# Pairing fewer edge chunks to a TensorE product in a graph layer, with two more spare products

## The chip, the cores and the metric

The kernel runs on one core of a Trainium2 chip. The metric is the device time of one execution in microseconds (us). Before the change, three runs took 308.38, 308.87 and 310.85 us; the median is 308.87. Engines are named as in the profile: PE is TensorE's matmul, PEld its weight load, DVE is VectorE, ACT is ScalarE, POOL is GpSimd, SP is SyncE.

## The reference

One layer of a graph network: 12,500 nodes of 128 numbers, 412,500 edges of 48 numbers, each edge added to its destination node, then a small MLP with a residual. The edges come sorted by destination.

```python
def reference(x, src, dst, edge_attr_48, graph_globals, W1, b1, W2, b2):
    h = jnp.maximum(_layernorm(x, axis=-1), 0.0)
    agg = jax.ops.segment_sum(edge_attr_48, dst, num_segments=12500)
    u = graph_globals[zeros(12500, int32)]
    z = jnp.concatenate([h, agg, u], axis=1)          # 128 + 48 + 64
    return x + jax.nn.relu(z @ W1 + b1) @ W2 + b2     # hidden 256
```

All is float32. Reading the edges' numbers takes most of the memory traffic: 412,500 x 48 x 4 bytes are 79 MB.

## The kernel before

**Steps.** The edges are cut into chunks of 896 (128 partitions x T = 7), and eight chunks make a step: two halves h of four chunks each. There are 58 steps, 0 to 57; the last has four chunks and a rest of 340 edges. Since the edges are sorted, the 896 destinations of a chunk lie within a window of 32 nodes. For each step VectorE builds a one-hot tile `oh` (`onehot`, line 290) that says for each edge which of the window's 32 nodes it belongs to, and `aggregate` (line 314) multiplies it with the edges on TensorE: for each of the seven t and each chunk one product of a 128x32 one-hot (the weights) with a 128x48 edge tile. The four chunks of a half write to four different groups of 32 of TensorE's columns. A step without pairs has 56 such products.

**Pairs, or levels.** `aggregate(s, h, twos)` can do the last `twos` of the seven t in another way: the one-hots of two neighbouring chunks, 64 columns, are the weights of one product, and both chunks' edges, 96 columns, stream through. Half of what comes out is of no use, the blocks off the diagonal. One such t is called a level here. A level takes two products in place of four, and each of them streams twice as many columns. Only the half h = 1 is ever paired. A step with at least one level needs two more copies in `keep_sums` (line 335), since the odd chunks' sums of that half then lie beside the even ones'; a step with no level needs one copy on ScalarE.

A product is recorded in the trace as two weight loads and two matmuls, as are the other float32 products.

**Loads.** Each step's edges come in four loads of two chunks, 336 KB, issued by SyncE (`load`, line 279), three steps ahead. `few` (line 272) lets at most FLIGHT = 5 loads (edges, node blocks and destinations) be under way, and also makes each load wait for the last TensorE product placed ahead of it in the program.

**The other work of a step.** `place` and `add` (lines 358 and 366) put a step's window sums, two steps later, at their nodes in the array `aggT`. The node blocks of 512 go through LayerNorm, a transposition (`turn`, `keep`), the two halves of the first product (`first_h`), its share from the aggregated edges (`first_a`), ReLU, the second product (`second`), the residual (`result`) and a store. These pieces are placed by hand in half steps k = 2s and 2s + 1 (`at`, `piece`), each with a reckoned TensorE time that `work[k]` adds up. The order on every engine is the order in which the program is written (`manual_schedule`).

**How many levels.** For each step, lines 770 to 777 reckon two times: `us`, the time that TensorE streams (1.75 plus the step's `work`, plus 0.08 for each level), and EACH_US for each product. `n` counts the products of the step, all kinds (57 to 70 before any pairing). Levels are added while the first time is the lower one, up to seven; the last four steps have none.

**Spare products.** `spare` (line 593) is a 128x128 by 128x512 product of constants whose result nobody reads. Two are issued before step 0, and one each in the half steps k = 1 and k = 3, that is, in steps 0 and 1.

**Order within a step** (lines 743 to 786): `place`, first load, pieces of 2s, second load, `add`, pieces of 2s + 1, third load, the aggregation of both halves, fourth load, `keep_sums`, and on VectorE the column positions of step s and the one-hots of step s + 2.

Of the kernel before, what the change touches and what calls it, by code (L numbers as in the profile page):

```python
# [22 lines left out]
def kernel(  # L23
# [117 lines left out]
    with fast:  # L141
# [34 lines left out]
        def product(*a, **k):  # L176
            count[0] += 1
            last[:] = [nc.tensor.matmul(*a, **k).ins.name]  # L178
# [100 lines left out]
        def load(s, i):  # L279
            if s >= NS or s == NSF and i > 1:  # L280
                if s == NSF and i == 2:
                    edges[s].append(etail)
                return
            for c in (2 * i,):
                e = ep.tile([P, 2, T * DE], F32, name="e")
                few(load_edges(e, s * CS + c, 2))
                edges.setdefault(s, []).extend([e[:, 0], e[:, 1]])
                both.setdefault(s, []).append(e)

        def onehot(s):  # L290
            oh = ohp.tile([P, CH, T, 2, W], F32, name="oh")

            def compare(to, n, r):
                nc.vector.tensor_tensor(  # L294
                    to, iota[:, None, :W].to_broadcast([P, n, W]), r[:, :, None].to_broadcast([P, n, W]), OP.is_equal)

            def chunks(a, b):
                compare(oh[:, a // 2:b // 2].rearrange("p c t u w -> p (c t u) w"), (b - a) * T,
                        rel[:, (s * CS + a) // 2:(s * CS + b) // 2].rearrange("p c t u -> p (c t u)"))

            if s == NSF:
                chunks(0, CH)
                compare(oh[:, CH // 2, :TT, 0], TT, relt[:, :TT])
            elif s < 2:
                chunks(0, CH)
                chunks(CH, CS)
            else:
                chunks(0, CS)
            onehots[s] = oh
# [4 lines left out]
        def aggregate(s, h, twos):  # L314
            left = s == NSF and h
            if h == 0:
                banks_s[s] = ps_agg.tile([P, 512], F32, name="ps")[:, :4 * DE].rearrange("p (h f) -> p h f", h=2)
            ps, es, oh = banks_s[s], edges[s], onehots[s]
            n = TT if left else T
            for t in range(n):  # L320
                first, end = t == 0 and h == 0, t == n - 1
                if t >= n - twos:
                    for q in range(0, CH, 2):
                        c = CH * h + q
                        product(ps[W * q:W * (q + 2), h], oh[:, c // 2, t], both[s][c // 2][:, :, t * DE:(t + 1) * DE],
                                start=first, stop=end, skip_group_check=True)
                    continue
                for q in range(1 if left else CH):
                    c = CH * h + q
                    o = DE * (q % 2) if twos else 0  # L330
                    product(
                        ps[W * q:W * (q + 1), h, o:o + DE], oh[:, c // 2, t, c % 2], es[c][:, t * DE:(t + 1) * DE],
                        start=first, stop=end, skip_group_check=True)

        def keep_sums(s, twos):
            ps = banks_s.pop(s)
            to = sums[s % NSB].rearrange("p h (u f) -> p h u f", u=2)[:, :, :, :DE]

            def keep_these(k, h, o):
                nc.scalar.copy(to[k, h], ps[k, h, None, o:o + DE].to_broadcast(  # L340
                    [k.stop - k.start, h.stop - h.start, 2, DE]))

            if s < NSF:
                keep_these(slice(0, P), slice(0, 2), 0)
            else:
                keep_these(slice(0, P), slice(0, 1), 0)
                keep_these(slice(0, W), slice(1, 2), 0)
            hs = [h for h in range(2) if twos[h]]
            for q in range(1, CH, 2) if hs else ():
                keep_these(slice(W * q, W * (q + 1)), slice(hs[0], hs[-1] + 1), DE)  # L350

        def place_columns(s):
            po = ohp.tile([P, 2, WP], F32, name="place")
            nc.vector.tensor_tensor(po, iota[:, None, :WP].to_broadcast([P, 2, WP]),  # L354
                                    pos[:, s, :, None].to_broadcast([P, 2, WP]), OP.is_equal)
            places[s] = po

        def place(s):
            banks_p[s] = pp = ps_p.tile([P, 512], F32, name="pp")
            po = places.pop(s)  # L360
            for h in range(2):
                k = W if s == NSF and h else P
                product(pp[:HI + DE, SECOND * h:SECOND * h + WP], sums[s % NSB][:k, h, :HI + DE], po[:k, h],
                                 start=(h == 0), stop=(h == 1), skip_group_check=True)

        def add(s):
            _, v = nc.values_load_multi_w_load_instructions(
                at_i[0:1, s:s + 1], engines=[DVE], min_val=low(s), max_val=high(s),
                skip_runtime_bounds_check_because="clamped to these on the chip")
            to = aggT[:, ds(v[0], WG)]  # L370
            nc.vector.tensor_tensor(to, to, banks_p.pop(s)[:HI + DE, :WG], OP.add)  # L371
# [186 lines left out]
        with tc.manual_schedule():  # L558
# [71 lines left out]
            def at(k, f, *a):  # L630
                todo.setdefault(max(0, k), []).append((f, a))


            def placed(s):
                return min(s + 2, max(LATE, s + 1))
# [48 lines left out]
            for j in range(NBL):  # L684
                k = where["turn", j]
# [13 lines left out]
            def apart(k, f, *a):  # L699
                while k - 1 in taken or k in taken or k + 1 in taken:  # L700
                    k -= 1
                taken.add(k)
                at(k, f, *a)
                return k
# [6 lines left out]
            at(6, middles, 1)  # L711
            at(10, check_dst, 0)
            at(12, check_dst, 1)
            for k in (1, 3):
                at(k, spare)
            for i in range(2, len(parts)):
                need = 2 * (parts[i][0] // CS - (4 if i == len(parts) - 1 else 0))
                k = apart(need - 4, middles, i)
                at(k + 2, check_dst, i)
                k = apart(k - 1, spread_dst, i, 1)  # L720
                k = apart(k - 1, spread_dst, i, 0)
# [5 lines left out]
            k = apart(2 * (NS - 6), verdict)  # L727
# [10 lines left out]
                at(where["turn", j], keep, j)  # L738
            assert placed(ready[x1]) < NS

            ALL, TURN, MORE, EACH_US = 1.75, 0.15, 0.08, 0.08
            counted = count[0]
            for s in range(NS):
                now = [p for p in range(NS) if placed(p) == s]
                paced[:] = [s] * (s > 0)

                def next_load(i):
                    if s > 0:
                        load(s + AHEAD - 1, i)

                if s < LATE:
                    for p in now:
                        place(p)
                next_load(0)
                for f, a in todo.pop(2 * s, []):
                    f(*a)
                next_load(1)
                if s < LATE:
                    for p in now:
                        add(p)  # L760
                for f, a in todo.pop(2 * s + 1, []):
                    f(*a)
                next_load(2)
                if s >= LATE:
                    for p in now:
                        place(p)
                        add(p)


                us = ALL + work.get(2 * s, 0.0) + work.get(2 * s + 1, 0.0)  # L770
                n, twos = count[0] - counted + CS * T, [0, 0]
                while us + TURN < EACH_US * n and twos[1] < T and s < NS - 4:
                    twos[1] += 1
                    us += MORE
                    n -= 2
                aggregate(s, 0, twos[0])
                aggregate(s, 1, twos[1])
                counted = count[0]
                next_load(3)
                keep_sums(s, twos)  # L780
                if s == 1:
                    place_columns(0)
                if s > 0:
                    place_columns(s)
                if s + EARLY < NS:
                    onehot(s + EARLY)
# [166 lines left out]
```

## Time and profile before

The profiled execution is one run under the hardware profiler.

| | |
|---|---|
| median of three runs | 308.87 us (308.38 to 310.85) |
| the profiled execution's own time | 310.81 us |
| its span in the trace | 309.1 us |
| mean granted TensorE clock | 0.994 of full speed |
| HBM read, written | 87.74 MB, 6.40 MB |
| packets of kind "instruction" on q8 | 51, 0.84 MB |
| edge loads | 230 |

Times in the trace count from the span's start. A row of the timeline merges neighbouring instructions of a kind: start, length, engine and line, names and shape of the first, and their number; in square brackets stands the engine's idle time ahead of it and what ended it. In the groups by line, the columns after the count are busy time, mean length of one in ns, and the idle time ahead with its releasers. "issue" is idle time for which the profile shows no wait. In windows, each engine has its busy time and number of instructions, and the last three columns are the granted clock, the share of time that the 16 DMA engines are busy, and GB/s. Nearly all products on the chip come through one helper, line 178, so groups are told apart by their tiles: `ps<-e,oh` is the aggregation, `pp<-place,sums` the placing, `ph` the first product, `po` the second, `pt` the transpositions.

Where the steps lie: step 24's aggregation starts at 129.30 us, step 51's at 264.31, step 53's at 273.75, step 57's at 293.24.

### The profile page before, as it was taken

How to read it: one execution, taken by the hardware profiler on the slowest of the kernel's cores; microseconds unless marked ns; L12 is line 12 of the kernel's file. 1: busy time of each engine (PE TensorE's matmuls, PEld its weight loads, DVE VectorE, ACT ScalarE, POOL GpSimd, SP SyncE). 2: the span in 40 equal slices, each digit the busy share in tenths (PEclk: the TensorE clock that was granted, in tenths of full speed). 3: DMA queues.
4: the chain of work that ended last, by engine and by line, in shares of the span. 5: the costliest groups of instructions: out<-in, count | busy, mean ns of one | idle time of the engine just before them, and what ended most of it. 6: DMA issues, size and time to landing. Idle time of an engine off the chain costs nothing. (4 is left out here: it accounts for less than half of the span.)

```text
span 309.1 us, 14799 instructions
## 1 busy us (share of the span) xinstructions
PE 291.4 (94%) x6397; PEld 227.5 (74%) x6398; DVE 231.8 (75%) x530; ACT 164.1 (53%) x426; POOL 78.5 (25%) x87
## 2 busy tenths in 40 slices
PE   7888999999999999989999999999999899999982
PEld 3577767767877877866877887876887777786772
DVE  6867958987695967759976598779984899797221
ACT  2223696465564764645454487655452884665320
POOL 8221041032120544222134204123303033223000
PEclk9997999999999999999999999999999999999999
DMA  7999999999999999999999999999999999998102
GB/s 231 313 322 316 338 338 336 343 361 296 336 344 333 365 349 331 312 333 287 319 354 326 363 335 333 346 348 322 315 367 312 289 354 321 375 357 279 39 0 75
DMA packets 69717, 95.15 MB, mean 308 GB/s; under 512 B 5018, under 2 KB 64611, under 8 KB 69647
## 3 DMA queue, kind: packets, MB, share of 16 engines
q1 hardware_dynamic: 67439, 87.53, 85.3%
q0 software_dynamic: 2208, 6.63, 5.6%
q8 instruction: 51, 0.84, 1.1%
q14 instruction: 19, 0.16, 0.1%
HBM read 87.74 MB, written 6.40 MB: 305 GB/s over the span
## 5 line engine op out<-in xcount | busy, mean ns | idle before, releaser
L178 PE MATMUL ps<-e,oh 128*32 128x48 f32 (+1 forms) x5288 | 117.6, 218 | 7.2 <-issue 4.6
L178 PEld LDWEIGHTS ps<-e,oh 128*32 128x32 f32 (+1 forms) x5288 | 100.7, 116 | 31.4 <-issue 10.2
L294 DVE TENSOR_TENSOR oh<-iota,rel 128x1792 f32<-128x1792 f32 (+1 forms) x60 | 116.0, 1936 | 0.0
L340 ACT COPY sums<-ps 128x192 f32<-128x192 f32 (+1 forms) x165 | 43.1, 262 | 97.5 <-PE ps L178 94.9
L497 POOL DMA_DIRECT2D out_dram<-ot x25 | 14.0, 560 | 207.9 <-DVE ot L489 156.1
L371 DVE TENSOR_TENSOR aggT<-aggT,pp 112x246 f32 x58 | 23.7, 409 | 39.6 <-PE pp L178 30.3
L411 POOL TENSOR_TENSOR xb<-xt,b_sb 128x512 f32<-128x512 f32 (+2 forms) x26 | 46.5, 1792 | 15.3 <-DMA xt<-in_x_dram 9.8
L178 PE MATMUL po<-w,hid 128*128 128x128 f32 (+1 forms) x384 | 47.7, 276 | 1.3 <-ACTq L815 1.3
L178 PE MATMUL ph<-hT,w1h 128*128 128x512 f32 (+2 forms) x100 | 47.5, 578 | 0.6 <-ACT hT L432 0.6
L178 PEld LDWEIGHTS po<-w,hid 128*128 128x128 f32 (+1 forms) x384 | 44.9, 191 | 2.2 <-ACTq L815 1.4
L475 ACT ACTIVATE hid<-ph,bias 128x512 f32<-128x512 f32 (+2 forms) x49 | 30.4, 670 | 24.5 <-PE ph L178 23.3
L418 ACT ACTIVATE xn<-xt,sh,sc 128x128 f32<-128x128 f32 (+1 forms) x98 | 40.5, 483 | 0.5
L178 PE MATMUL pp<-place,sums 128*112 128x128 f32 x232 | 39.7, 295 | 0.0
L178 PEld LDWEIGHTS pp<-place,sums 128*112 128x112 f32 x232 | 29.2, 178 | 7.6 <-issue 1.5
L354 DVE TENSOR_TENSOR place<-iota,pos 128x256 f32<-128x256 f32 x58 | 34.3, 593 | 0.0
L178 PE MATMUL ph<-aggT,w1a 48*128 48x256 f32 (+1 forms) x192 | 28.3, 400 | 0.0
L432 ACT COPY hT<-pt 128x512 f32<-128x512 f32 (+2 forms) x26 | 26.7, 1026 | 3.1 <-PE pt L182 3.1
L489 DVE TENSOR_TENSOR ot<-po,xb 128x512 f32<-128x512 f32 (+2 forms) x25 | 16.6, 665 | 13.5 <-PE po L178 12.2
L178 PEld LDWEIGHTS ph<-aggT,w1a 48*128 48x128 f32 x192 | 17.3, 186 | 10.9 <-issue 7.8
L388 DVE BATCH_NORM_STATS2 st<-xt 128x6 f32<-128x128 f32 (+1 forms) x98 | 21.3, 279 | 1.8 <-DMA xt<-in_x_dram 1.8
L178 PEld LDWEIGHTS ph<-hT,w1h 128*128 128x128 f32 x100 | 16.2, 191 | 6.4 <-issue 3.3
L182 PE MATMUL pt<-ident,xn 128*128 128x128 f32 (+1 forms) x98 | 15.9, 282 | 0.0
(120 smaller groups left out, 139.7 us busy)
## 6 DMA issues: line engine op xcount, KB each, us to landing
e<-in_edge_attr_dram SPq DMA_DIRECT2D x230, 336.0 KB, 5.1
xt<-in_x_dram SPq DMA_DIRECT2D x23, 256.0 KB, 4.8
out_dram<-ot POOLq DMA_DIRECT2D x23, 256.0 KB, 5.5
di<-in_dst_dram SPq DMA_DIRECT2D x3, 448.0 KB, 6.9
xt<-in_x_dram SPq DMA_DIRECT2D x2, 128.0 KB, 4.2
out_dram<-ot SPq DMA_DIRECT2D x2, 128.0 KB, 2.6
di<-in_dst_dram SPq DMA_DIRECT2D x1, 154.0 KB
w1h<-in_L_gnn_W_dram POOLq DMA_DIRECT2D x1, 128.0 KB, 5.6
```

What stands on the lines that cost most here:

```text
L178: last[:] = [nc.tensor.matmul(*a, **k).ins.name]
L182: last[:] = [nc.tensor.transpose(*a, **k).ins.name]
L294: nc.vector.tensor_tensor(to, iota[:, None, :W].to_broadcast([P, n, W]), r[:, :, None].to_broadcast([P, n, W]), OP.is_equal)
L340: nc.scalar.copy(to[k, h], ps[k, h, None, o:o + DE].to_broadcast([k.stop - k.start, h.stop - h.start, 2, DE]))
L354: nc.vector.tensor_tensor(po, iota[:, None, :WP].to_broadcast([P, 2, WP]), pos[:, s, :, None].to_broadcast([P, 2, WP]), OP.is_equal)
L371: nc.vector.tensor_tensor(to, to, banks_p.pop(s)[:HI + DE, :WG], OP.add)
L388: nc.vector.bn_stats(st[:m, q, :], xs[j][:m, q, :])
L411: nc.gpsimd.tensor_tensor(xb[:m, :r], xs[j][:m, :r], b2_sb[:m, None, :].to_broadcast([m, r, D]), OP.add)
L418: nc.scalar.activation(xn[:m, q], xs[j][:m, q], AF.Relu, bias=shift[j][:m, q:q + 1], scale=scale[j][:m, q:q + 1])
L432: nc.scalar.copy(hT[:, :m * r].rearrange("d (p r) -> d r p", r=r), ht[j][:, :m * r].rearrange("d (r p) -> d r p", r=r))
L475: nc.scalar.activation(to, ph, AF.Relu, bias=bias[:, h:h + 1])
L489: nc.vector.tensor_tensor(ot[:m, :r], pos_o[j][:m, :r], xbs[j][:m, :r], OP.add)
```

## The change

```diff
@@ the spare products
-            for k in (1, 3):
+            for k in range(1, 8, 2):
                 at(k, spare)
@@ the plan of levels
-            ALL, TURN, MORE, EACH_US = 1.75, 0.15, 0.08, 0.08
+            ALL, TURN, MORE, EACH_US, FEW = 1.75, 0.15, 0.08, 0.073, 3
...
                 us = ALL + work.get(2 * s, 0.0) + work.get(2 * s + 1, 0.0)
                 n, twos = count[0] - counted + CS * T, [0, 0]
                 while us + TURN < EACH_US * n and twos[1] < T and s < NS - 4:
                     twos[1] += 1
                     us += MORE
                     n -= 2
+                if twos[1] < FEW:
+                    twos[1] = 0
                 aggregate(s, 0, twos[0])
                 aggregate(s, 1, twos[1])
```

The reckoned time of a product falls from 0.080 to 0.073 us, so that a step asks for fewer levels. A step that asks for one or two gets none. Spare products also go into the half steps 5 and 7, that is, steps 2 and 3. What is loaded, computed and stored stays the same, and so does every other piece's place.

## The prediction

> **What bounds the kernel now.** I read the page first: busy shares, slices, queues.
>
> ```profile
> span 309.1 us, 14799 instructions
> PE 291.4 (94%) x6397; PEld 227.5 (74%) x6398; DVE 231.8 (75%) x530; ACT 164.1 (53%) x426; POOL 78.5 (25%) x87
> PEclk9997999999999999999999999999999999999999
> DMA  7999999999999999999999999999999999998102
> q8 instruction: 51, 0.84, 1.1%
> e<-in_edge_attr_dram SPq DMA_DIRECT2D x230, 336.0 KB, 5.1
> ```
>
> TensorE is busy for 94% of the span, and the DMA engines are full in nearly every slice up to the 37th of 40, which ends at 286 us. Two resources are full at once, so the question is which one waits for the other. The groups by line, the windows, SyncE's own waits and the general waits answer that.
>
> ```profile
> L178 PE MATMUL ps<-e,oh 128*32 128x48 f32 (+1 forms) x5288 | 117.6, 218 | 7.2 <-issue 4.6 <-DMA e<-in_edge_attr_dram 2.5
> L340 ACT COPY sums<-ps 128x192 f32<-128x192 f32 (+1 forms) x165 | 43.1, 262 | 97.5 <-PE ps L178 94.9
> 180.00:220.00 40.00, 39.45 (x884) 31.19 (x880) 33.51 (x72) 24.37 (x62) 9.06 (x8) 1.00 1.01 338
> SPq L127 <- DMA e<-in_edge_attr_dram: 116.4, 179, 3.0
> SPq L127 <- PE pp L178: 5.7, 20, 0.4
> ```
>
> The loads run on their own clock. At most five are in flight (FLIGHT, line 556); five of 336 KB (344,064 bytes), landing in 5.1 us, make 337 GB/s, and the window from 180 to 220 us shows 338 with a DMA share of 1.01. SyncE waits for an earlier load 179 times, 116.4 us in all; its most frequent wait for TensorE is 20 times, never over 0.4 us. So a quicker TensorE does not make the edges arrive sooner. TensorE's aggregation in turn stood only 2.5 us on a missing load. Both streams move at nearly the same pace.
>
> At the end they part. The timeline of SyncE and TensorE there:
>
> ```profile
> 256.42 24.50 SPq L127 DMA_DIRECT2D e<-in_edge_attr_dram  x24
> ...
> 264.31 1.95 PE L178 MATMUL ps<-e,oh 128*32 128x48 f32 x92
> ...
> 273.75 2.11 PE L178 MATMUL ps<-e,oh 128*32 128x48 f32 x84
> 275.79 2.05 PE L178 MATMUL po<-w,hid 128*128 128x128 f32 x16
> ...
> 279.06 1.40 PE L178 MATMUL ps<-e,oh 128*32 128x48 f32 x112
> 280.39 1.13 PE L178 MATMUL ph<-hT,w1h 128*128 128x512 f32 x2
> ...
> 283.54 0.54 PE L178 MATMUL ps<-e,oh 128*32 128x48 f32 x30
> ...
> 284.64 1.12 PE L178 MATMUL ps<-e,oh 128*32 128x48 f32 x82 [0.56 <-issue]
> ...
> 293.24 0.80 PE L178 MATMUL ps<-e,oh 128*32 128x48 f32 x56
> ```
>
> The first row holds the last 24 of the 230 loads, one each 1.02 us. Four belong to a step and two to the last step, so number 207, issued at 256.42, is the third of step 51, and the fourth goes about 1.0 us later. With 5.1 us to landing the two are there at 261.5 and 262.5. TensorE begins step 51's products at 264.31. It needs the third and fourth load only for the half h=1, about 0.7 us into the block, so it could have begun at 261.8. It is 2.5 us behind the loads. The last load goes at about 256.4 + 24.5 = 280.9 and lands near 286, but step 57's products start at 293.24: after step 51 TensorE alone sets the end.
>
> **What the change does to TensorE's stream.** The plan (lines 741 to 785) can be worked out by hand. A common step has pieces of 2.68 us and 67 products. Its reckoned time is 1.75 + 2.68 = 4.43. Before, a level is added while the time + 0.15 is under 0.08 x products: 4.58 < 5.36, 4.66 < 5.20, 4.74 < 5.04, 4.82 < 4.88, then no more, so four levels. After, the bound is 0.073 x products: 4.58 < 4.89, 4.66 < 4.75, then no more. Two are under three, so none. Over the 58 steps this gives 288 levels in 53 steps before and 180 in 36 after. Of the 108 levels lost, 62 go from 17 steps that fall to none, and 46 from other steps, one to two levels each. Two of my counts have a check in rows above: 57 x 56 + 28 + 4 = 3224 products unpaired less 2 x 288 are 2648, four of them on the tail's own tile, and 2644 x 2 records are the 5288 shown; ACT's copies are 58 + 1 + 2 x 53 = 165.
>
> A level's price comes from three blocks with 84, 96 and 112 records, that is seven, four and no levels (56 products less two a level, two records each). The first and the last stand above. The four-level one, step 24, and the block after it:
>
> ```profile
> 129.30 1.87 PE L178 MATMUL ps<-e,oh 128*32 128x48 f32 x96
> 131.10 0.69 PE L178 MATMUL pp<-place,sums 128*112 128x128 f32 x4
> 131.63 1.02 PE L178 MATMUL ph<-hT,w1h 128*128 128x512 f32 x2
> 132.58 1.14 PE L178 MATMUL ph<-aggT,w1a 48*128 48x256 f32 x8
> 133.65 0.66 PE L182 MATMUL pt<-ident,xn 128*128 128x128 f32 x4
> 134.24 0.79 PE L178 MATMUL ps<-e,oh 128*32 128x48 f32 x53
> 135.94 1.34 PE L178 MATMUL ps<-e,oh 128*32 128x48 f32 x43 [0.92 <-issue]
> ```
>
> From a block's start to the next operation are 275.79 - 273.75 = 2.04 us with seven levels, 131.10 - 129.30 = 1.80 with four, and 280.39 - 279.06 = 1.33 with none. So a level costs TensorE 0.08 us (0.24 over three), and a block without any saves 0.15 more (0.47 over four levels). The stream gets shorter by 108 x 0.08 + 17 x 0.15 = 8.6 + 2.6 = 11.2 us.
>
> **What it adds: instructions.** Each lost level is two products more, 216 in all, and a product is two weight loads and two matmuls: 864 instructions, and 8 for the two spare products. The page has 6397 + 6398 such records against 51 packets of the kind "instruction" on q8, about 251 records and 16 KB to a packet; 872 more need about 3.5 packets more. That these packets can hold TensorE up is seen in the last fence: step 25's block stops for 0.92 us on "issue", that is, on nothing that the profile shows. The answer for 133.5 to 136.0 us, around that stop, counts one such packet, and the one for 131.0 to 133.5 none:
>
> ```profile
> q8 instruction: 1, 0.02, 2.3%
> ```
>
> ```profile
> 240.72 1.67 PE L178 MATMUL ps<-e,oh 128*32 128x48 f32 x51 [0.96 <-issue]
> PE ps L178 <- issue: 4.6, 9, 1.0
> ```
>
> In all the aggregation loses 4.6 us in nine stops. Without pairs a step of 67 products holds 268 instructions, more than one packet, 224 of them in 1.33 us, so every one of the 17 steps meets the end of a packet, many inside the dense block. What a step loses to this lies between nothing and the longest stop, 0.96 us (more instructions give no gain). Steps 52 and 54 to 57 already run without pairs and had one stop, 0.56 us (284.64): 0.11 a step. But their last ones run as the loads thin out, so I take 0.3, nearer to the tail's value than to the 0.96: 17 x 0.3 = 5.1 us. TensorE then gains 11.2 - 5.1 = 6.1 us gross (range: 11.2 down to 11.2 - 16.3 = -5.1).
>
> The Trainium skill, page "Runtime: NRT & Kernel Launch", section "Instruction fetch mechanics", says that instructions come in 16 KiB blocks of 256, that the next is fetched while the current one executes, and that crossing a boundary is mostly hidden. The packet size agrees; the stops of 0.92 and 0.96 us do not. By that rule alone the new instructions would be free, which is the first rival below.
>
> **How much of it reaches the end.** Not 6.1 us: up to step 51 TensorE can only close up on loads that do not come sooner. The most that can count is the 2.5 us by which it trails them there, and 0.08 from step 53 (seven levels to six): 2.6 us. Of that something is lost to stops too late to be made up. The surplus on the loads is small (6.1 us over some 46 steps, 0.13 a step), so a stop like that of 0.96 at 240.72, five steps ahead of step 51, is still mostly there, and steps 45 and 50, both newly without pairs, bring 0.3 each: 0.96 + 0.6 = 1.6 us. Left: 1.0 us.
>
> **What costs nothing.** ACT makes two copies fewer in 17 steps, 34 x about 0.26 = 8.9 us; its copies wait 94.9 us for TensorE, so nobody waits for them. The two spare products go into steps 2 and 3, late in each, ahead of its block and of its third load's place in the order:
>
> ```profile
> 13.92 1.13 PE L178 MATMUL ph<-iota,ones 128*128 128x512 f32 x2
> 14.97 1.49 PE L178 MATMUL ps<-e,oh 128*32 128x48 f32 x58
> ...
> 20.61 1.37 PE L178 MATMUL ps<-e,oh 128*64 128x96 f32 x26 [0.51 <-DMA e<-in_edge_attr_dram]
> ...
> 24.76 0.38 PE L178 MATMUL ps<-e,oh 128*64 128x96 f32 x2 [0.33 <-DMA e<-in_edge_attr_dram]
> 25.72 2.50 PE L178 MATMUL ps<-e,oh 128*64 128x96 f32 x26 [0.58 <-DMA e<-in_edge_attr_dram]
> ...
> 31.61 1.37 PE L178 MATMUL ps<-e,oh 128*64 128x96 f32 x26 [0.54 <-DMA e<-in_edge_attr_dram]
> ```
>
> One takes 14.97 - 13.92 = 1.05 us, two 2.1. TensorE waits for loads there 0.51 + 0.33 + 0.58 + 0.54 = 1.96 us, and the block at 25.72 takes 1.13 us longer than its like at 20.61, in the fourth slice, whose granted clock is 0.7 on the page; more work may hold it up: 3.1 us of cover. If the cover were gone, 2.1 us would push the steps behind, and the wait at 31.61 shows the loads still last there, so step 4 takes that up. The two loads of a step that are paced by the spare product (line 277) wait longer for an earlier load anyway.
>
> **The rivals.**
> *The instructions come free.* For it: the blocks at 279.06 and 293.24 ran without pairs and without a stop. Against it: nine stops before, with thinner blocks. Then the whole 2.6 us count: 308.87 - 2.6 = 306.3.
> *The supply of instructions becomes the bound: slower.* Place: the 17 steps without pairs. A four-level step with 67 products takes 134.24 - 129.30 = 4.94 us, and 4.47 without pairs if nothing stops it. If TensorE gets a packet's 64 products only every 5.1 us (0.08 us a product, the value the plan had), the step takes 67 x 0.08 = 5.36, 0.42 worse, and 17 x 0.42 = 7.1 us less the 46 x 0.08 = 3.7 of the other steps is 3.4 us slower: 312.3. It decides from 4.94 x 64 / 67 = 4.7 us a packet. For it: the stops near 1 us. Against it: step 54 went from 279.06 to 283.54, 4.48 us for 67 products, with loads still running.
> *Nothing moves.* The loads or stops take all back: 308.9.
> That the plan does something else is excluded by the changed program's list of products, where steps stand with 56 unpaired.
>
> **How the numbers follow.** The profiled execution took 310.81 us, 1.7 beyond its span, at the upper edge of the runs (308.38 to 310.85, median 308.87). The sum, made on it, is 310.81 - 1.0 = 309.8; its difference applied to the median gives 307.9, the forecast, with 0.5. Its own range is 306.6 to 309.2. Free instructions 0.17, supply-bound 0.2 (taking in milder forms from 309.5 on), nothing moves 0.13. The range, with two in ten outside, is 306.0 to 311.2. A measurement can tell about 1% from no change: faster means below 305.8, past the 2.6 us that the loads allow, so only a quicker load stream gives it: 0.08. Slower means above 312.0: 0.14, most of the supply rival. The same: 0.78.
>
> **What would show it.** Groups: 5288 + 432 = 5720 records of ps, 12 of the spares, 131 copies; q8 at 54 or 55. "PE ps <- issue" should grow from 4.6 us to 8 to 11, and TensorE's waits for e with it, as it closes up. Step 51's block should begin 0.5 to 2 us earlier against its loads, and the loads' last issue stay at 281. Wrong would be: a last load clearly earlier or later (the loads are not independent), issue stops unchanged (free instructions), or blocks without pairs that stop in nearly every step (supply-bound).

## The result: 2.7% slower

The changed kernel takes 319.03 us (median of six runs, 316.99 to 322.02) against 311.05 us (six runs, 308.38 to 312.48) for the kernel before. The ratio is 1.027, with a 95% interval of 1.020 to 1.033; it is that of the mean times, with one slow run of the changed kernel, 322.02, left out. The forecast was 307.9 and its range ended at 311.2. The rival in which the supply of instructions becomes the bound had the right sign, at 312.3, less than half the loss.

The page of the profile after, with the lines that answer to those shown of before:

```profile
span 317.1 us, 15643 instructions
PE 287.0 (91%) x6833; PEld 222.2 (70%) x6834; DVE 233.6 (74%) x530; ACT 155.0 (49%) x392; POOL 76.1 (24%) x87
PEclk9999999999999999999999999959999999999998
q8 instruction: 55, 0.90, 1.2%
L178 PE MATMUL ps<-e,oh 128*32 128x48 f32 (+1 forms) x5720 | 108.6, 215 | 14.6 <-issue 12.0
```

TensorE has 436 matmul records more and is busy 4.4 us less (291.4 before), in a span that is 8.0 us longer: it stands still more. The aggregation's idle time on "issue" went from 4.6 to 12.0 us. The waits for TensorE as a whole and SyncE's own:

```profile
PE ps L178 <- issue: 12.0, 12, 1.7
PE ph L178 <- issue: 2.3, 2, 1.3
PE pp L178 <- issue: 2.0, 1, 2.0
PE po L178 <- issue: 1.1, 1, 1.1
```

```profile
SPq L127 <- DMA e<-in_edge_attr_dram: 104.3, 157, 2.6
SPq L127 <- PE ps L178: 12.8, 14, 3.8
```

Matmuls that stand on "issue" come to 17.4 us in 16 stops; before there were nine, all in the aggregation. And the loads now wait for TensorE's aggregation 12.8 us, up to 3.8 us at a time. The same row of before, and the last 24 loads of after:

```profile
SPq L127 <- PE ps L178: 1.8, 8, 0.3
```

```profile
255.96 30.11 SPq L127 DMA_DIRECT2D e<-in_edge_attr_dram  x24
```

The 24 loads begin where they began before, at 256 us, and take 30.11 us in place of 24.50, so the last one goes at about 286 us in place of 281. TensorE fell behind the loads. Its own waits for edges did not grow (2.4 us, 2.5 before).

One stretch of the timeline, steps 38 and 39, shows the worst stop:

```profile
201.08 1.40 PE L178 MATMUL ps<-e,oh 128*32 128x48 f32 x112
202.41 0.36 PE L178 MATMUL pp<-place,sums 128*112 128x128 f32 x1
204.76 0.49 PE L178 MATMUL pp<-place,sums 128*112 128x128 f32 x3 [1.99 <-issue]
205.09 1.33 PE L178 MATMUL ph<-hT,w1h 128*128 128x512 f32 x2
206.35 2.08 PE L178 MATMUL ph<-aggT,w1a 48*128 48x256 f32 x8
208.36 1.11 PE L182 MATMUL pt<-ident,xn 128*128 128x128 f32 x4
209.40 2.47 PE L178 MATMUL ps<-e,oh 128*32 128x48 f32 x112
```

A block without pairs runs at full speed, 1.33 us from its start to the next operation, and one record after it TensorE stands for 1.99 us. What follows is slow: the same block at 209.40 takes 2.47 us for 1.40, the eight records of `ph` 2.08 us for 1.14. The windows give the granted clock, the third number from the right:

```profile
196.00:204.00 8.00, 6.77 (x223) 5.67 (x218) 6.44 (x15) 4.39 (x11) 2.66 (x2) 1.00 0.99 332
204.00:212.00 8.00, 7.24 (x130) 4.89 (x130) 4.17 (x8) 2.50 (x5) 0.41 (x1) 0.60 0.92 308
```

The clock falls to half after the stop and stays there for 6.8 us by the trace's clock records.

### The profile page after: what moved, and what is told of

It reads as the page before. It is cut to its first block, busy times and chain, and to the rows that moved or that the text cites. A ratio compares the mean times of both kernels' runs of the same rounds, so it can differ in the third digit from the quotient of the medians.

```text
span 317.1 us, 15643 instructions
## 1 busy us (share of the span) xinstructions
PE 287.0 (91%) x6833; PEld 222.2 (70%) x6834; DVE 233.6 (74%) x530; ACT 155.0 (49%) x392; POOL 76.1 (24%) x87
## 5 line engine op out<-in xcount | busy, mean ns | idle before, releaser
L178 PE MATMUL ps<-e,oh 128*32 128x48 f32 (+1 forms) x5720 | 108.6, 215 | 14.6 <-issue 12.0
L178 PEld LDWEIGHTS ps<-e,oh 128*32 128x32 f32 (+1 forms) x5720 | 93.4, 115 | 39.5 <-issue 19.8
L340 ACT COPY sums<-ps 128x192 f32<-128x192 f32 (+2 forms) x131 | 35.3, 270 | 104.2 <-PE ps L178 102.3
L411 POOL TENSOR_TENSOR xb<-xt,b_sb 128x512 f32<-128x512 f32 (+2 forms) x26 | 44.2, 1704 | 14.8 <-DMA xt<-in_x_dram 8.9
L354 DVE TENSOR_TENSOR place<-iota,pos 128x256 f32<-128x256 f32 x58 | 35.7, 616 | 0.0
L178 PE MATMUL ph<-aggT,w1a 48*128 48x256 f32 (+1 forms) x192 | 29.8, 412 | 2.3 <-issue 2.3
L178 PEld LDWEIGHTS ph<-aggT,w1a 48*128 48x128 f32 x192 | 18.3, 192 | 13.8 <-issue 10.6
```

The source lines that it names most:

```text
L411: nc.gpsimd.tensor_tensor(xb[:m, :r], xs[j][:m, :r], b2_sb[:m, None, :].to_broadcast([m, r, D]), OP.add)
```

## Where the time went, by a sum over the steps

Undisturbed pieces take the same time to about 0.01 us in all the kernels of the table: a block without levels 1.33 us, with two 1.64, four 1.80, seven 2.04, and the other work of a kind of step likewise. So the time from the start of step 5's aggregation to that of step 57's can be split in two: the stream (the undisturbed lengths added up) and what lies above it. One profile each, in us, worked out from the traces; "instructions" is the difference to the kernel before on TensorE, four a product, and "issue" the waits of all matmuls on issue over the whole span.

```
kernel            instructions  levels   stream  above it   issue (stops)   ratio to before (95%)
before                     0      288    250.5      7.0       4.6 (9)
changed                 +872      180    239.3     26.9      17.4 (16)     1.027 (1.020 to 1.033)
changed, again          +872      180    239.3     24.6      14.3 (18)     1.025 (1.015 to 1.036)
dense_only              +496      226    243.0     19.4      11.9 (16)     1.012 (1.004 to 1.020)
each_only               +640      208    243.8     18.9      14.6 (15)     1.008 (0.999 to 1.016)
even182                 +856      182    241.7     21.8      13.7 (21)     1.013 (1.008 to 1.019)
even182, again          +856      182    241.7     13.9       9.9 (11)     1.013 (1.005 to 1.020)
more_pairs              -512      352    255.7      2.6       1.5 (3)      1.010 (1.005 to 1.014)
merge_a                 -184      288    250.5      8.1       6.7 (8)      1.003 (0.999 to 1.007)
```

The change saved the 11.2 us of stream that were forecast and paid 19.9 us (17.6 in the second profile) above it. Within that part of the span the waits on issue grew from 4.3 to 17.4 us, by 13.1; the half clock of 6.8 us can add some 3.4 us (an estimate: half of that time). The rest is not accounted for one by one.

The stops have a signature. Number all of TensorE's instructions in the trace from 0: weight loads, matmuls and the rest, mostly waits on semaphores. Then the first instruction behind each of the changed kernel's 16 stops, a matmul or its weight load, has a number that leaves 193 when divided by 256. The same holds for all stops in the table's other profiles, though their products lie at other places. Each of the 16 ends 2.2 to 2.6 us after a 16 KB packet of kind "instruction" begins to move. So a stop is TensorE at the end of one packet's 256 instructions, waiting for the next. In the changed kernel the next packet begins to move 2.5 us (median) after TensorE has entered the one before, in the kernel before 2.2 us; with the some 2.4 us to its first use that makes 4.5 to 5 us to get 256 instructions. This time varies: at the 16 stops it was 4.5 to 7.0 us, with a median of 5.7.

Where the stops stand is not where the pairs went. Only 5 of the 16, 6.1 us, lie in the 17 steps that fell to none, and all of these come at the end of the dense block or behind it. From one aggregation's start to the next, those 17 steps together take 0.8 us more than before (0.8 less in the second profile), and the 35 other steps between 5 and 57 take 8.0 us more (7.3). Five of the stops in other steps stand in the step right behind one of the 17, so a step may use up a packet and leave the wait for the next one to the step behind it.

## Experiments

Theory S: the change makes TensorE use its instructions faster than packets of them come. Rival F: instructions come free, and the loss is in something else (spare products, clock, thinner pairs). Later S was split: S1, their number counts; S2, it counts how fast a single packet is used up.

**One part at a time.** dense_only:

```diff
+                if s in (6, 8, 9, 11, 13, 18, 20, 24, 25, 26, 32, 33, 38, 39, 40, 45, 50):
+                    twos[1] = 0
                 aggregate(s, 0, twos[0])
```

> The kernel before with one part of the change alone: the 17 steps that the change leaves without pairs have none, all other steps keep their levels (288 to 226 levels), no new spare products. Theory S (supply of instructions): 124 products more are 496 more TensorE instructions, all in dense blocks; the stops on issue in the aggregation grow from 4.6 us to 9 us or more, the stream saves only 17 x 0.31 to 0.47 = 7.5 us, and the time is 1 to 2% above the kernel before. Rival F (instructions come free, the slowdown is from something else, the spare products or the lower clock): 0.5 to 0.8% faster than before, stops unchanged.

315.16 us, ratio 1.012 (1.004 to 1.020): slower, as S has it, and the stops grew as forecast. The stream is 7.5 us shorter, the time above it 12.4 us longer.

```profile
PE ps L178 <- issue: 10.3, 14, 1.5
```

each_only:

```diff
-            ALL, TURN, MORE, EACH_US = 1.75, 0.15, 0.08, 0.08
+            ALL, TURN, MORE, EACH_US = 1.75, 0.15, 0.08, 0.073
```

> The kernel before with 0.073 in place of 0.080 us a product alone: 208 levels in 51 steps, no step set to none, no new spare products. It has 160 products more than before, 56 fewer than after, and the 17 steps keep one or two levels each. Theory S: still short of instructions, stops of 7 to 10 us, 0.5 to 1.5% slower than before. If setting the 17 steps to none is what hurts, apart from the number of instructions: equal to before within 0.3%. Rival F: 0.5 to 0.8% faster.

314.88 us, ratio 1.008 (0.999 to 1.016). The stops are above the forecast 7 to 10 us; the time is where S put it, its interval just reaching no change.

```profile
PE ps L178 <- issue: 12.9, 14, 2.2
```

spares_only:

```diff
-            for k in (1, 3):
+            for k in range(1, 8, 2):
```

> The kernel before with the two new spare products in steps 2 and 3 alone. Theory S and the prediction: within 0.4% of before, since the loads are last there; the granted clock stays full around 26 us where the kernel before shows a stretch at half. Rival (the spares push the early steps and this is never made up): 2 us or 0.7% slower.

311.74 us, ratio 1.001 (0.993 to 1.009): the spare products cost nothing that shows, and F loses that place. Around 26 us the clock is full, as expected, but not all along: the trace has half clock from about 15 to 18 us and from 32 to 35 us, the fifth slice of the page here (31 to 39 us) reading 0.7.

```profile
PEclk9989799999999999999999999999999999999999
```

**Do packets wait behind the loads?** after_flight3, the changed kernel:

```diff
-        FLIGHT = 5
+        FLIGHT = 3
```

> The changed kernel with at most 3 loads under way in place of 5. Theory S with the fetch waiting behind loads in the DMA engines: packets of instructions start sooner, stops fall from 12 us to 7 or less and TensorE closes up on the loads; if 3 loads still fill the DMA engines (load stream as long as before, last issue near 285 us), the time falls by 1.5 to 3% against the changed kernel, to 309 to 314 us. If the time to get a packet doesn't depend on the loads: stops stay at 12 us and the time is that of the changed kernel. If 3 loads are too few: TensorE waits for e over 10 us and the time is above 320.

389.31 us, ratio 1.25 (1.241 to 1.259): three loads are too few. The loads, in the page's part on DMA issues:

```profile
e<-in_edge_attr_dram SPq DMA_DIRECT2D x230, 336.0 KB, 4.2
```

and TensorE's waits:

```profile
PEld ps L178 <- DMA e<-in_edge_attr_dram: 67.8, 71, 2.5
```

A load lands in 4.2 us, less by 1.1 than the 5.3 with five in flight, so three bring 3 x 0.344 MB / 4.2 us = 246 GB/s. TensorE then waits for edges and has no stop on issue, so the time says nothing on packets. The trace says a little: the next packet begins to move 1.3 us (median) after TensorE enters one, against 2.5 in the changed kernel with five loads. That speaks for packets that wait behind loads, but TensorE's waits for edges shift the moment from which this is counted, so it is not shown. flight7, the kernel before with FLIGHT = 7, asks from the other side:

> The kernel before with 7 loads under way in place of 5. If a packet of instructions waits its turn behind the loads in the DMA engines, more loads in flight make every packet later: stops on issue grow from 4.6 to over 9 us and the time by 1 to 3%, while the loads come no faster, the engines being full already. If packets don't wait behind loads: stops and time as before, within 0.3%.

310.47 us, ratio 0.998 (0.994 to 1.002), 6.7 us of stops. SyncE's waits:

```profile
SPq L127 <- PE pp L178: 69.2, 76, 3.5
SPq L127 <- DMA e<-in_edge_attr_dram: 23.9, 45, 1.2
```

With seven allowed, the loads run up to where they must wait for TensorE, and the time does not move. The stops, 6.7 us, lie between the two forecasts, and the next packet begins to move 1.7 us (median) after TensorE enters one, not later than the 2.2 of before. So more loads in flight do not make the packets later by an amount that shows, and in the kernel before, too, it is TensorE, not the loads, that sets the time.

**The number of instructions with the stream held.** merge_a (the kernel before, levels written out as they were):

```diff
-            for q in range(0, n, 256):
-                w = min(256, n - q)
+            for q in range(0, n, 512):
+                w = min(512, n - q)
```

> The kernel before, with its levels held fixed, and each block's product with the aggregated edges done over 512 columns at once in place of twice 256: 46 products or 184 TensorE instructions fewer, the streamed columns the same. Theory S (time per instruction where the supply is short): from the first call the cost is about 11 to 23 ns an instruction (dense_only: 3.9 us slower with 7.5 us less stream for 496 instructions), so 2 to 4 us, of which the loads let about 2.5 us through: 0.5 to 0.8% faster than before, the stops fall below 4 us. Rival F (the number of instructions is not what counts, the thinner pairs are): equal within 0.2%.

312.72 us, ratio 1.003 (0.999 to 1.007): no gain. S as it stood, a price per instruction, missed.

split_h, its counterpart:

```diff
-            product(ph, w1h[:, h * P:(h + 1) * P], ht[j][:, :n], start=(h == 0 or not small),
-                             stop=False, skip_group_check=True)
+            for q in range(0, n, 256):
+                product(ph[:, q:min(q + 256, n)], w1h[:, h * P:(h + 1) * P], ht[j][:, q:min(q + 256, n)],
+                        start=(h == 0 or not small), stop=False, skip_group_check=True)
```

> The counterpart: the kernel before, its levels held fixed, and each block's first product over 256 columns twice in place of 512 once: 46 products or 184 TensorE instructions more, the streamed columns the same, and the weights of those products loaded twice. Nothing in the aggregation changes. Theory S: 2 to 4 us or 0.6 to 1.3% slower, and the stops on issue in the aggregation grow though the aggregation is untouched. Rival F: equal within 0.3%, stops as before.

313.81 us, ratio 1.010 (1.003 to 1.017). In this run part of the first product's sum is lost in the hidden layer; instructions and stream are as said. Slower as forecast, but not by the cause: the stops did not grow.

```profile
PE ps L178 <- issue: 3.2, 5, 1.0
```

In its profile the time above the stream from step 5 on is 7.1 us, as before, while step 5 itself begins 4 us later than in the kernel before, with the clock at half twice in the first 38 us. The run decides nothing for S.

after_merge_a, the same edit in the changed kernel:

> The changed kernel, its levels held fixed, with the same 184 instructions taken out as in merge_a. Theory S: 3 to 4 us faster than the changed kernel, a ratio to before of 1.013 to 1.020 where the changed kernel has 1.027. Rival F: 1.027.

313.76 us, ratio 1.010 (1.005 to 1.015), some 1.7% below the changed kernel. The same 184 instructions that were worth nothing in the kernel before are worth about 5 us here. Its one profile is of the longest of its ten runs, 319.79 us, with 13.2 us of stops, so where the 5 us were won is not shown.

more_pairs (0.09 for 0.08 us a product in the kernel before):

> The kernel before with 0.09 in place of 0.08 us a product: 352 levels in place of 288, 128 products or 512 instructions fewer, and a stream longer by 64 x 0.08 = 5.1 us. Theory S: stops on issue in the aggregation fall under 2 us, and time is within 0.7% of before, since most of the 5.1 us is won back. Rival F, or a kernel bound by the stream alone: 1.2 to 1.7% slower.

312.57 us, ratio 1.010 (1.005 to 1.014), between the two forecasts. The stops nearly vanish:

```profile
PE ps L178 <- issue: 1.5, 3, 0.9
```

By the table, one profile each, 5.2 us of stream were added and 4.4 us above it won back; the runs put the loss at about 3 us. The kernel before lies between a side that pays in stream and a side that pays in stops.

**How even the instructions lie.** spread (the kernel before, levels written out):

```diff
+                aggregate(s, 0, 0)
                 for f, a in todo.pop(2 * s + 1, []):
                     f(*a)
...
-                aggregate(s, 0, twos[0])
                 aggregate(s, 1, twos[1])
```

> The kernel before, its levels held fixed, with the half h=0 of each step's aggregation moved ahead of the pieces of the second half step, so that the densest run of instructions, 168 to 224 in one block, is cut in two with slower products between. Same instructions, same stream. Theory S2 (a stop comes when one packet's 256 instructions are used up sooner than the next packet comes; how evenly instructions are spread counts, not only how many): the time above the stream between steps 5 and 57, 7 us in the kernel before, falls to 3 to 5 us and the time by 0.3 to 0.8%. Theory S1 (only the number of instructions counts): equal within 0.3%.

The stops vanish, as S2 says: in 51 packets of instructions the matmuls have 0.3 us on issue left. The time does not follow: 315.16 us, ratio 1.012 (1.007 to 1.016). The engines' line of its page:

```profile
PE 301.2 (96%) x6397; PEld 231.7 (74%) x6398; DVE 231.1 (73%) x530; ACT 163.8 (52%) x426; POOL 77.6 (25%) x87
```

The timeline of one step with its two halves (start, time, instruction):

```profile
137.41 0.80 PE L178 MATMUL ps<-e,oh 128*32 128x48 f32 x56
138.15 0.66 PE L182 MATMUL pt<-ident,xn 128*128 128x128 f32 x4
138.73 1.27 PE L178 MATMUL ps<-e,oh 128*32 128x48 f32 x40
139.94 0.69 PE L178 MATMUL pp<-place,sums 128*112 128x128 f32 x4
```

TensorE is busy 301.2 us for 291.4. The two halves of a four-level step take 138.15 - 137.41 = 0.74 and 139.94 - 138.73 = 1.21 us, 1.95 together where the block in one piece took 1.80. A block cut in two costs 0.15 us, and over some 57 steps that is 8.6 us, more than all the stops were worth.

after_spread, the same move in the changed kernel:

> The changed kernel with the same move. S2: the 27 us above its stream fall to 20 or less, a ratio to before of 1.00 to 1.015. S1: 1.027 as the changed kernel.

319.91 us, ratio 1.026 (1.020 to 1.032): no faster than the changed kernel. Issue stops fell to 10.5 us from 17.4, and the longer stream took it back.

even182:

```diff
-            ALL, TURN, MORE, EACH_US, FEW = 1.75, 0.15, 0.08, 0.073, 3
+            ALL, TURN, MORE, EACH_US, FEW = 1.75, 0.15, 0.08, 0.0716, 0
```

> The changed kernel with 0.0716 us a product and no step set to none: 182 levels, 2 more than the changed kernel's 180, but spread over 51 steps where the changed kernel has 36. S2: fewer stops than the changed kernel for the same number of instructions, 20 to 24 us above the stream in place of 27, ratio 1.012 to 1.020. S1: ratio 1.027. This tells whether setting steps to none costs more than the instructions that it adds.

315.6 us, ratio 1.013 (1.008 to 1.019): its plan has 182 levels for 180, so with the two spares it has 214 products more than the kernel before, 856 instructions for the changed kernel's 872, and about half its loss. Its stream is 2.4 us longer than the changed kernel's. So setting steps to none costs beyond the number of instructions. Its profile has no half clock in the middle, where the changed kernel's had 5.3 us above the stream in steps 38 and 39. Whether that was chance was asked on one chip:

> The changed kernel once more, for a second profile beside even182_again on one chip. In its first profile one stop of 1.99 us was followed by 6.8 us at half the granted clock, and the steps in it lost 5.3 of the 27 us above the stream. If the lower clock belongs to the change's cost, a stretch at half clock in the middle of the span shows again and the ratio stays near 1.027; if it was chance, the second profile has none there, some 22 us above the stream, and a span near 313.

> The kernel with 182 levels spread over 51 steps, once more, on the same chip as after_again. S2 (setting steps to none costs beyond the instructions): 0.7 to 1.5% below after_again. S1: within 0.4% of it.

318.39 us, ratio 1.025 (1.015 to 1.036), against 313.21 us, ratio 1.013 (1.005 to 1.020): the difference stands, and so does the stop. In the second profile of the changed kernel it is at the same place in step 38, one record into the placing:

```profile
199.93 1.40 PE L178 MATMUL ps<-e,oh 128*32 128x48 f32 x112
201.26 0.36 PE L178 MATMUL pp<-place,sums 128*112 128x128 f32 x1
203.89 0.49 PE L178 MATMUL pp<-place,sums 128*112 128x128 f32 x3 [2.27 <-issue]
```

Half clock follows again, for 3.4 us, and that step loses 4.1 us. The spread between executions is large: even182's own two profiles have 21.8 and 13.9 us above the stream.

merge_a_flight7, both edits, was the one candidate to beat both kernels:

> The kernel before with 184 instructions fewer (as merge_a) and 7 loads under way (as flight7). If the kernel before is held by its stream of 250 us and some 7 us of stops, and neither loads nor the number of instructions outside the dense blocks counts: within 0.4% of before. If loads held merge_a's gain back: 0.5 to 1% faster, which would beat both kernels.

311.31 us, ratio 1.002 (0.999 to 1.006). It was not the loads that held merge_a's gain back, and nothing here beats the kernel before.

## Why the prediction was wrong

The parts that held: the blocks of the changed kernel take the lengths that the prediction used, so the stream became 11.2 us shorter. The spare products cost nothing that shows. That ACT's 34 copies fewer (131 copies after) gave nothing was not tried alone, but dense_only has them too and is slower. The packets of instructions rose to 55, and the groups to 5720 records. The loads did not come sooner. "PE ps <- issue" was to grow to 8 to 11 us and reached 12.0; TensorE's waits for edges, which were to grow with it, did not.

The step that failed is the price of a stop: "I take 0.3, nearer to the tail's value than to the 0.96: 17 x 0.3 = 5.1 us". Measured from step 5 to 57 the time above the stream grew by 19.9 us, in the second profile by 17.6. Three things in that step were off. The price was put on the 17 steps alone, and the cost in all other steps was put at nothing. With the 7.5 us of stream that the 17 steps save, the time above it grew there by 8.3 us (6.7 in the second profile); in the other steps it grew by 11.6 us (11.0). All steps that lost one or two levels use their packets faster too: each_only and even182, which leave nearly no step without pairs, have 19 and 14 to 22 us above the stream. The upper bound, the longest stop of before, was no bound: stops of 1.99 and 2.27 us came, and half the clock behind each for 6.8 and 3.4 us. And the lower gauge, the tail's 0.11 us a step, was taken where loads thin out and only five steps lie.

The step behind it, that only 2.6 us could reach the end because of the loads, had nothing to act on and was not tried: TensorE did not close up on the loads, it fell back until they waited for it (12.8 us of SyncE's waits on `ps`).

Of the rivals, the free instructions fall: dense_only, each_only and even182 all have a shorter stream and a longer time. The supply rival named the mechanism and its sign. Its price, 0.42 us in 17 steps less 3.7 us, assumed that the other steps keep their gain of 0.08 a level; they did not, and it knew nothing of the clock. Its threshold was near the mark: 4.47 us for a step of 268 instructions is under the 4.5 to 5 us that a packet typically takes to come, and the 4.94 us of a four-level step with 236 instructions, 5.4 us a packet, is just over it. But its sign, blocks without pairs that stop in nearly every step, did not come: the stop stands where a packet ends, often in a later block.

How the loss divides: the ratio of 1.013 for even182 is what the added instructions cost where they lie evenly, and the other 1.2% (1.025 against 1.013 on one chip) is what setting 17 steps to none adds. Some 4 to 5 us of that second part lie in the two profiles in steps 38 and 39, in the stop and the half clock behind it. How much of the rest is in longer stops stays open, since the profiles of one kernel differ by up to 8 us above the stream. Why a packet comes early at one time and late at another, and whether loads in flight are the reason, stays open too.

## What to carry to other kernels

An engine fed with many short instructions has a second limit beside its stream: here 256 TensorE instructions typically came per 4.5 to 5 us, and per 5.7 us where TensorE stopped, and a plan that shortens the stream by using more instructions stops paying where a packet is used up faster than that. Look for "issue" waits in the trace, and see whether they end at equal distances in instructions and at a fixed time after an instruction packet; if so, price them over all steps by the time per packet, not by the stops seen so far: here 872 instructions more took them from 4.6 to 17.4 us. Look for a stop's cause in the instructions ahead of it, since it stands where a packet ends and not where the instructions were added. The same instructions were worth nothing in one kernel (merge_a) and 1.7% in the other (after_merge_a), so a price per instruction does not carry over.

## What was not expected of the hardware

One stop of about 2 us in an otherwise full stream was followed by half the granted clock for 3.4 and 6.8 us, in both profiles of the changed kernel. It is no rule: each_only has a stop of 2.16 us, and the clock stays full behind it:

```profile
147.37 1.35 PE L178 MATMUL ps<-e,oh 128*32 128x48 f32 x45 [2.16 <-issue]
147.50:152.00 4.50, 4.50 (x116) 4.20 (x116) 2.59 (x15) 1.87 (x4) 0.00 (x0) 1.00 0.90 282
```

In after_merge_a's profile two stops of 2.01 and 2.06 us have 3.4 us of half clock behind them. What decides it is open. Cutting a block of products on column groups in two cost 0.15 us, by which the removal of nearly all stops was lost. And with three loads in flight in place of five a load of 336 KB landed in 4.2 us for 5.3, only a fifth sooner, so the loads' rate fell by a quarter.
